# Grouping GpSimd's weight additions and tying each group to a point of VectorE's work

## The chip, the cores and the metric

The kernel runs on one core of a Trainium2 chip. The metric is the device time of one execution in microseconds (us); several executions of a kernel are timed and their median is taken. The engines of a core are TensorE (PE in the profile, with its weight loads as PEld), VectorE (DVE), ScalarE (ACT), GpSimd (POOL) and the DMA issuer SyncE (SP). They run side by side, each in the order of its own program, and wait for each other only where the data require it.

## What is computed

For x of shape 2 x 2048 x 512 in float32, two layers follow each other, cut here to what matters:

```python
def dense(x, wi, wo): return relu(x @ wi) @ wo          # 512 -> 2048 -> 512
s0, s1 = dense(x, swi[0], swo[0]), dense(x, swi[1], swo[1])
eo     = dense(x, wi[type_label], wo[type_label])       # weights picked per batch row
w      = softmax(relu(concat(eo[:,0], s0[:,0], s1[:,0]) @ g1) @ g2)
x      = x + eo*w[0] + s0*w[1] + s1*w[2]
out    = x + (x @ W[cat_ids] + b[cat_ids])
```

## The kernel before

**Units.** The tokens are cut into four blocks of 1024. A unit is one block with one pair of weights (one expert): four blocks with shared expert 0 (units 0 to 3), four with shared expert 1 (units 4 to 7), and four with the two experts that the labels pick (units 8 to 11; two blocks each). Each unit has an up part (x times wi, L755) and a down part (h times wo, L886).

**Seven products in place of eight.** Both parts are done as a two-level Strassen-Winograd scheme: seven outer products, and in each of them seven inner ones. This saves matmuls, and needs sums of quarters of the operands in exchange. An up product has 14 slots (`SEQ_UP`) of two matmuls, in the order i = 1, 6, 2, 5, 7, 4, 3; the down part has 49 slots (`SLOTS_DN`) of four matmuls, in the order i = 1, 2, 3, 7, 6, 5, 4. A slot's name such as "x6" or "y5" gives the accumulation bank (x, y or z) and the inner product that is added to it.

**Who makes the sums.** VectorE adds the results of the banks together, since the scheme's outputs are sums of partial results (L772, L778, L783, L796, L802 in the up part; L900, L908, L910, L917, L919 in the down part). These read one operand from the accumulation banks and one from SBUF. It also makes the sums of the hidden values: `wide` (L733) and `make_tops` (L690 to L697) in the up part, `outer_sum` (L857), `make_tops` and `y_sums` (L863) in the down part; these read both operands from SBUF. GpSimd makes the sums of x for the next products (`x_sums`, L356 and L370, in the up parts of units 0 to 4 and the ends of the down parts before them), and the sums of the weights of the next experts.

**The weight additions.** Class `Prep` makes the weight sums of one expert and one kind (up or down weights). There are six such objects (experts 1 to 3, two kinds), and each works in four groups of twelve additions (`line`, issued at L141): four of 128x384 elements for tile `po`, four of 128x512 for `ps`, four of 128x512 for `pt`. So there are 288 additions. A group's raw weights are loaded into one buffer by eight DMAs on SP's queue (L179); each finished tile is stored to DRAM by SP three slots later (`flush`, L228), and fetched as weight tiles by later units through a ring of twelve buffers (`fetch_w`, `wp`).

**The pacing.** The program is written out slot by slot. At the end of each slot, `prep_paced` (L637) advances a clock and adds a rate to a balance, and for each whole unit of the balance it issues one weight addition into GpSimd's program:

```python
        pace[0] = min(pace[0] + rate, 4.0) if prep_bg else 0.0
        while prep_bg and pace[0] >= 1 and prep_step():
            pace[0] -= 1
    ...
    RATE_UP = [0.36, 0.34, 0.34, 0.34, 0.18, 0.18, 0.34]
    RATE_DN = {1: 0.0, 2: 0.0, 3: 0.1, 7: 0.4, 6: 0.0, 5: 0.25, 4: 0.45}
```

This sets the order within GpSimd's program and the place of the raw loads and stores in SP's program. It does not bind the additions to VectorE or TensorE in time: an addition starts as soon as GpSimd reaches it and its operands are there. Other work that is issued at each slot's end stands beside it: `advance(xg, 1)` (x sums, before the pacing in the same slot), `next(tg, None)` and `next(job, None)` (VectorE's sums).

Of the kernel before, what the change touches and what calls it, by code (L numbers as in the profile page):

```python
# [8 lines left out]
F32 = mybir.dt.float32  # L9
# [10 lines left out]
ADD, SUB = ALU.add, ALU.subtract  # L20
# [16 lines left out]
def cond_resid_kernel(  # L37
# [22 lines left out]
    nc = tc.nc  # L60
# [10 lines left out]
    const = ctx.enter_context(tc.tile_pool(name="const", bufs=1))  # L71
# [72 lines left out]
    class Prep:  # L144
# [89 lines left out]
        def step(self):  # L234

            self.flush(clock[0])
            done = bool(self.p) and (len(self.p) != 12 or clock[0] >= self.since + 6)
            if done:
                self.p.pop(0)()
            self.more()  # L240
            return done

        def more(self):
            if self.reading == 0 and (not self.p or clock[0] >= self.free):
                self.begin()
# [86 lines left out]
    def fetch_parts(n, i):  # L332

        t = xp.tile([P, NP, TQ], F32, tag="xr", name=f"xs_{n}_{i}")
        nc.sync.dma_start(out=t, in_=xs[units[n][1]][:, i - 1])
        for k in PART_B:
            x_ops[n, i, k] = t[:, PART_B[k], :]
# [99 lines left out]
    clock = [0]  # L437
# [175 lines left out]
    def used_w():  # L613
        w_used[0] += 1
        fetch_w(w_used[0] + 12)
# [3 lines left out]
    prep_bg, other_bg = [], []  # L619
# [9 lines left out]
    def prep_step():  # L629
        done = prep_bg[0].step()  # L630
        if prep_bg[0].over():
            prep_bg.pop(0)
        return done

    pace = [0.0]

    def prep_paced(rate):  # L637
        clock[0] += 1
        if prep_bg:
            prep_bg[0].flush(clock[0])  # L640
        pace[0] = min(pace[0] + rate, 4.0) if prep_bg else 0.0
        while prep_bg and pace[0] >= 1 and prep_step():
            pace[0] -= 1

    def advance(gen, count=None):

        while count is None or count > 0:
            mark = next(gen, "next")
            if mark:
                return True  # L650
            if count is not None:
                count -= 1
        return False
# [6 lines left out]
    def blk_of(t, cc):  # L660

        r, q = INNER[cc]
        o = (r * 2 + q) * 1024
        return t[:, o : o + 1024].rearrange("p (g t) -> p g t", g=NG)
# [35 lines left out]
    def up(n, xg, tops, y):  # L700
# [12 lines left out]
        for j, i in enumerate(I_UP(n)):  # L713
# [11 lines left out]
            def relu(q, cc):  # L725
                v = blk_of(O[q], cc)
                nc.scalar.activation(v, v, AF.Relu)  # L727

            def wide(q, cc):


                o = blk_of(O[q], cc)
                nc.vector.tensor_tensor(o, blk_of(O[22], cc), blk_of(O[21], cc), ADD)  # L733
                if q == 22:
                    relu(22, cc)
# [6 lines left out]
            done = False  # L742
# [3 lines left out]
            for s, (bk, k, d) in enumerate(SEQ_UP):  # L746
                first = (bk, k) in (("x", 1), ("y", 5))
                if first:
                    bank[bk, d] = ps.tile(
                        [P, 2, TQ], F32, tag=bk, name=f"u{bk}_{n}_{i}_{d}"  # L750
                    )
                p = bank[bk, d]
                wt = w_tiles[n, 0, i, k]
                for g in range(2):
                    nc.tensor.matmul(  # L755
                        p[:, g, :],
                        lhsT=wt[:, 2 * d + g, :],
                        rhs=x_ops[n, i, k],
                        start=first and g == 0,
                        stop=True,  # L760
                        skip_group_check=True,
                    )
                if all(kk != k for _, kk, _ in SEQ_UP[s + 1 :]):
                    used_w()
                if k == 1:
                    z = bank["z", d] = ps.tile(
                        [P, 2, TQ], F32, tag="z", name=f"uz_{n}_{i}_{d}"
                    )
                    if store:
                        nc.scalar.activation(z, p, AF.Copy)  # L770
                    else:
                        nc.vector.tensor_tensor(z, p, half(src, 11, d), ADD)  # L772
                elif bk == "x" and k in SNAP:
                    t = snp.tile([P, 2, TQ], F32, tag="sn", name=f"us_{n}_{i}_{k}_{d}")
                    if store:
                        nc.scalar.activation(t, p, AF.Copy)  # L776
                    else:
                        nc.vector.tensor_tensor(  # L778
                            t, p, half(src, 12 if k == 6 else 22, d), ADD
                        )  # L780
                    sn[SNAP[k], d] = t
                    if k == 7:
                        nc.vector.tensor_tensor(  # L783
                            half(dst, 22, d), bank["y", d], t, ADD
                        )
                        if d == 1 and i in final:
                            relu(dst, 22)
                elif bk == "z":
                    nc.scalar.activation(  # L789
                        half(dst, 11, d), p, AF.Relu if i in final else AF.Copy  # L790
                    )
                elif k == 4:
                    if store:
                        nc.scalar.activation(half(dst, 21, d), p, AF.Copy)
                    else:
                        nc.vector.tensor_tensor(  # L796
                            half(dst, 21, d), p, half(src, 21, d), ADD
                        )
                    if d == 1 and i in final:
                        relu(dst, 21)  # L800
                elif k == 3:
                    nc.vector.tensor_tensor(half(dst, 12, d), p, sn["b", d], ADD)  # L802
                    if d == 1 and i in final:
                        relu(dst, 12)
                if s in wides:
                    wide(*wides[s])
                if n == 0 and i == 2:

                    for cc in {1: (11, 22), 2: (21,), 3: (12,)}.get(s, ()):
                        nc.scalar.activation(blk_of(O[21], cc), blk_of(O[11], cc), AF.Copy)  # L810
                if n == 0:
                    begin.outer({(1, 0): (5,), (1, 2): (6,), (2, 2): (7,), (6, 2): (3,)}.get((i, s), ()))
                    if (i, s) == (2, 2):
                        begin.second()
                    elif (i, s) == (7, 3):
                        begin.outer2(2)
                if xg and j < 6 and not done and (
                    s >= 7 if i in (7, 4) else s % 2 == 0 or j == 0
                ):
                    done = advance(xg, 1)  # L820
                if s in top_at:
                    next(tg, None)
                prep_paced(RATE_UP[j])
                step(other_bg)
                if s == 4 and n not in MAKES and j + 2 < NP:
                    fetch_parts(n, I_UP(n)[j + 2])
# [8 lines left out]
    def down(n, H, tops, y, prepare):  # L835
# [24 lines left out]
        def y_sums(m2, *pairs):  # L860
            for q, r in pairs:
                o = quad_of(y, q)[:, m2, :]
                nc.vector.tensor_tensor(o, o, quad_of(y, r)[:, m2, :], ADD)  # L863
# [96 lines left out]
        for s, (i, name) in enumerate(SLOTS_DN):  # L960
            if s in at:
                for _ in job:
                    pass
                job = jobs[at[s]]()
                y_sums(0, *sums.get(at[s], ()))
            elif s in second:
                y_sums(1, *sums.get(second[s], ()))
            slot(i, name)
            next(job, None)
            if name == "z2" and i != 1:  # L970
                next(job, None)
            prepare(s)
            prep_paced(RATE_DN[i])
            step(other_bg)
        for _ in job:
            pass
# [192 lines left out]

    RATE_UP = [0.36, 0.34, 0.34, 0.34, 0.18, 0.18, 0.34]
    RATE_DN = {1: 0.0, 2: 0.0, 3: 0.1, 7: 0.4, 6: 0.0, 5: 0.25, 4: 0.45}

    with tc.manual_schedule():

# [15 lines left out]
        for n, (e, blk) in enumerate(units):  # L1192
# [4 lines left out]
            if n:  # L1197
                y = yp.tile([P, DC, 4, TQ], F32, tag="y", name=f"y_{n}")
            H = up(n, xg, tops, y)
            coming = {}  # L1200

            def prepare(s, n=n, y=y):
# [30 lines left out]
                elif s in (30, 38):  # L1233
                    fetch_parts(m, I_UP(m)[(s - 30) // 8])

            down(n, H, tops, y, prepare)
            if n + 1 < len(units):
                xg = coming.get("s")
# [45 lines left out]
```

## Time and profile before

| | |
|---|---|
| median of three executions | 2267.57 us (2265.73 to 2278.35) |
| the profiled execution | 2271.67 us |
| its span in the profile | 2269.9 us |
| PE busy | 2200.9 us (97%) |
| DVE busy | 1662.7 us (73%) |
| POOL busy | 790.4 us (35%) |
| granted TensorE clock, mean | 0.994 |
| weight additions (L141) | 288, in units 0 (end) to 8 |

The profiled execution took 2271.67 us, 1.8 us more than its span and 4.1 us more than the median. A busy time is the sum of an engine's instructions; in a list of waits, the engine on the left stood still for what is on the right. In a list by form, "x16 | 19.2, 1217" means sixteen instructions, 19.2 us of busy time, 1217 ns for one on average. In a timeline, a line may merge several instructions; its two numbers are the start and the duration in us.

### The profile page before, as it was taken

How to read it: one execution, taken by the hardware profiler on the slowest of the kernel's cores; microseconds unless marked ns; L12 is line 12 of the kernel's file. 1: busy time of each engine (PE TensorE's matmuls, PEld its weight loads, DVE VectorE, ACT ScalarE, POOL GpSimd, SP SyncE). 2: the span in 40 equal slices, each digit the busy share in tenths (PEclk: the TensorE clock that was granted, in tenths of full speed). 3: DMA queues.
4: the chain of work that ended last, by engine and by line, in shares of the span. 5: the costliest groups of instructions: out<-in, count | busy, mean ns of one | idle time of the engine just before them, and what ended most of it. 6: DMA issues, size and time to landing. Idle time of an engine off the chain costs nothing.

```text
span 2269.9 us, 28541 instructions
## 1 busy us (share of the span) xinstructions
PE 2200.9 (97%) x9808; PEld 1852.3 (82%) x9808; DVE 1662.7 (73%) x2010; ACT 545.0 (24%) x937; POOL 790.4 (35%) x598
## 2 busy tenths in 40 slices
PE   7899999999999999899999999999999999999999
PEld 6787888888888888788888888888877877887676
DVE  7798687577598688588588588577676746857685
ACT  3221231331321231141131131131133133213310
POOL 5777642651751752333054134230032023002300
PEclk9999999999999999999999999999999999999999
DMA  9543997997996897796896896896896697579671
GB/s 320 213 148 110 334 337 219 327 310 231 329 329 207 285 330 213 255 323 200 284 327 178 280 327 207 280 327 174 283 312 187 185 301 244 153 242 326 208 273 56
DMA packets 479691, 577.22 MB, mean 254 GB/s; under 512 B 28216, under 2 KB 311864, under 8 KB 475580
## 3 DMA queue, kind: packets, MB, share of 16 engines
q1 hardware_dynamic: 475276, 567.53, 77.5%
q10 hardware_dynamic: 4272, 7.87, 1.0%
q8 instruction: 80, 1.31, 0.2%
q14 instruction: 63, 0.52, 0.1%
HBM read 417.47 MB, written 157.81 MB: 253 GB/s over the span
## 4 chain that ended last, share of the span: by engine, by line
PE 77%; DVE 14%; DMA 4%; issue 2%; POOL 2%; SPq 1%; ACT 0%; DVEq 0%; POOLq 0%; ACTq 0%
PE ux L755 21%; PE dx L886 20%; PE dy L886 10%; PE uy L755 10%; PE dz L886 5%; PE uz L755 5%; PE po L1066 5%; DVE h L857 2%; DVE h L733 2%; DVE y L863 1%; DVE t L690 1%; DVE t L695 1%; DVE t L693 1%; DMA g1raw<-in_L_cond_g_dram 1%; DMA y<-in_L_cond_swi_dram 1%
## 5 line engine op out<-in xcount | busy, mean ns | idle before, releaser
L886 PE MATMUL dx<-t,w 128*128 128x256 f32 x1680 | 399.0, 380 | 10.2 <-DVE ds L908 9.9
L755 PE MATMUL ux<-xs,w 128*128 128x256 f32 x1568 | 376.7, 381 | 11.4 <-DVE sm L1029 3.2
L886 PEld LDWEIGHTS dx<-t,w 128*128 128x128 f32 x1680 | 318.1, 190 | 58.6 <-DVE ds L908 12.3
L755 PEld LDWEIGHTS ux<-xs,w 128*128 128x128 f32 x1568 | 295.1, 190 | 67.8 <-DVE us L778 8.3
L1103 POOL TENSOR_TENSOR mix<-mix 128x512 f32<-128x512 f32 x72 | 101.9, 1416 | 532.9 <-DMA w<-ws_t 325.6
L141 POOL TENSOR_TENSOR po<-pr 128x384 f32<-128x384 f32 x48 | 58.9, 1241 | 601.4 <-DMA w<-ws_t 269.2
L778 DVE TENSOR_TENSOR us<-ux,h 128x512 f32<-128x512 f32 x240 | 162.5, 686 | 122.1 <-PE ux L755 121.8
L857 DVE TENSOR_TENSOR h<-h,h 128x1024 f32<-128x1024 f32 x192 | 251.2, 1323 | 0.0
L727 ACT ACTIVATE h<-h 128x1024 f32<-128x1024 f32 x156 | 164.5, 1056 | 245.1 <-DVE h L783 111.1
L783 DVE TENSOR_TENSOR h<-uy,us 128x512 f32<-128x512 f32 x168 | 116.0, 691 | 121.4 <-ACT us L776 117.0
L755 PE MATMUL ux<-xi,w 128*128 128x256 f32 x808 | 194.2, 384 | 9.6 <-issue 3.5
L789 ACT ACTIVATE h<-uz 128x512 f32<-128x512 f32 x168 | 99.6, 593 | 378.7 <-PE uz L755 354.5
L755 PE MATMUL uy<-xs,w 128*128 128x256 f32 x784 | 187.7, 380 | 2.7 <-DVE h L802 2.4
L755 PEld LDWEIGHTS ux<-xi,w 128*128 128x128 f32 x808 | 153.8, 192 | 36.5 <-issue 8.3
L886 PE MATMUL dy<-h,w 128*128 128x256 f32 x672 | 162.3, 385 | 12.1 <-DVE y L910 12.1
L755 PEld LDWEIGHTS uy<-xs,w 128*128 128x128 f32 x784 | 148.4, 190 | 29.1 <-DVE h L802 5.1
L886 PEld LDWEIGHTS dy<-h,w 128*128 128x128 f32 x672 | 128.2, 192 | 32.9 <-DVE y L910 10.4
L733 DVE TENSOR_TENSOR h<-h,h 128x1024 f32<-128x1024 f32 x96 | 148.3, 1545 | 6.7 <-ACT h L789 5.4
L802 DVE TENSOR_TENSOR h<-uy,us 128x512 f32<-128x512 f32 x168 | 113.0, 687 | 51.6 <-PE uy L755 49.4
L886 PE MATMUL dz<-h,w 128*128 128x256 f32 x616 | 145.6, 379 | 0.1
L886 PE MATMUL dx<-h,w 128*128 128x256 f32 x616 | 145.5, 379 | 0.0
L886 PE MATMUL dy<-t,w 128*128 128x256 f32 x576 | 136.1, 379 | 0.0
(153 smaller groups left out, 3359.1 us busy)
## 6 DMA issues: line engine op xcount, KB each, us to landing
w<-ws_t SPq DMA_DIRECT2D x352, 256.0 KB, 4.4
w<-ws_s SPq DMA_DIRECT2D x270, 256.0 KB, 4.2
w<-ws_o SPq DMA_DIRECT2D x264, 256.0 KB, 5.0
xs<-xs SPq DMA_DIRECT2D x49, 896.0 KB, 6.9
ws_s<-ps SPq DMA_DIRECT2D x24, 1024.0 KB, 9.9
ws_t<-pt SPq DMA_DIRECT2D x24, 1024.0 KB, 7.7
ys<-y SPq DMA_DIRECT2D x11, 2048.0 KB, 8.7
ws_o<-po SPq DMA_DIRECT2D x24, 768.0 KB, 7.5
```

The source lines that it names most:

```text
L141: eng.tensor_tensor(o, i0, i1, op)
L727: nc.scalar.activation(v, v, AF.Relu)
L733: nc.vector.tensor_tensor(o, blk_of(O[22], cc), blk_of(O[21], cc), ADD)
L755: nc.tensor.matmul(p[:, g, :], lhsT=wt[:, 2 * d + g, :], rhs=x_ops[n, i, k], start=first and g == 0, stop=True, skip_group_check=True,)
L778: nc.vector.tensor_tensor(t, p, half(src, 12 if k == 6 else 22, d), ADD)
L783: nc.vector.tensor_tensor(half(dst, 22, d), bank["y", d], t, ADD)
L789: nc.scalar.activation(half(dst, 11, d), p, AF.Relu if i in final else AF.Copy)
L802: nc.vector.tensor_tensor(half(dst, 12, d), p, sn["b", d], ADD)
L857: nc.vector.tensor_tensor(bl(o), bl(i0), bl(i1), SUB)
L886: nc.tensor.matmul(p, lhsT=wt[:, g, :], rhs=op[g], start=first and g == 0, stop=True, skip_group_check=True,)
L1066: nc.tensor.matmul(po[t], lhsT=mixed[c], rhs=l1[blk][0][:, c, :], start=(c == 0), stop=(c == DC - 1),)
L1103: nc.gpsimd.tensor_tensor(m[:, 3, :, :], m[:, 3, :, :], m[:, j, :, :], ADD)
```

## The change

The pacing is split in two. `prep_tick` runs at every slot and only advances the clock and stores what is due. `prep_run` issues a group of additions at the slots that two tables name, and, if an addition can be issued, puts a one-element memset into VectorE's program first and a one-element addition that reads it into GpSimd's program. GpSimd's program is in order, so everything behind that small addition waits until VectorE has come to the memset. The memsets take turns over 64 columns of a tile. A balance (`debt`, at most 4) carries what could not be issued; a group holds at most one addition more than its table says.

```diff
+        def can(self):
+            return bool(self.p) and (len(self.p) != 12 or clock[0] >= self.since + 6)
...
-    pace = [0.0]
-
-    def prep_paced(rate):
+    PULSES = 64
+    pulse = const.tile([1, PULSES], F32, name="pulse")
+    seen = const.tile([1, 1], F32, name="seen")
+    pulses, debt = [0], [0]
+
+    def prep_tick():
         clock[0] += 1
         if prep_bg:
             prep_bg[0].flush(clock[0])
-        pace[0] = min(pace[0] + rate, 4.0) if prep_bg else 0.0
-        while prep_bg and pace[0] >= 1 and prep_step():
-            pace[0] -= 1
+
+    def prep_run(count):
+
+        if not prep_bg:
+            return
+        debt[0] = min(debt[0] + count, 4)
+        most = count + 1
+        ready = False
+        while prep_bg and debt[0] and most:
+            if prep_bg[0].can() and not ready:
+                k = pulses[0] % PULSES
+                pulses[0] += 1
+                mark = pulse[:, k : k + 1]
+                nc.vector.memset(mark, 0.0)
+                nc.gpsimd.tensor_tensor(seen, mark, mark, ADD)
+                ready = True
+            if not prep_step():
+                break
+            debt[0] -= 1
+            most -= 1
...
-                prep_paced(RATE_UP[j])
+                prep_tick()
+                prep_run(RUN_UP[j].get(s, 0))
...
-            prep_paced(RATE_DN[i])
+            prep_tick()
+            prep_run(RUN_DN.get((i, name), 0))
...
-    RATE_UP = [0.36, 0.34, 0.34, 0.34, 0.18, 0.18, 0.34]
-    RATE_DN = {1: 0.0, 2: 0.0, 3: 0.1, 7: 0.4, 6: 0.0, 5: 0.25, 4: 0.45}
+    RUN_UP = [{4: 3, 8: 2}] * 3 + [{4: 2, 8: 2}] * 4
+    RUN_DN = {(7, "y5"): 2, (5, "x6"): 2, (4, "x6"): 2, (4, "z2"): 1}
```

More of the change, by code (lines that the diff above doesn't have):

```diff
@@ L236, in step @@
             self.flush(clock[0])
-            done = bool(self.p) and (len(self.p) != 12 or clock[0] >= self.since + 6)
+            done = self.can()
             if done:
```

## The prediction

> **What bounds the kernel now.** First the page: the span, the busy times, and how PE stands to the span.
>
> ```profile
> span 2269.9 us, 28541 instructions
> PE 2200.9 (97%) x9808; PEld 1852.3 (82%) x9808; DVE 1662.7 (73%) x2010; ACT 545.0 (24%) x937; POOL 790.4 (35%) x598
> ```
>
> PE is the bound: all but 69 us of the span. The change touches no matmul, so what can be won is PE's idle time where weight additions run. I cut the span into the up and down parts of units 1 to 8 (221.5 to 1620.6 us) and asked for the busy times of each. Two rows, unit 4's down part and unit 8's (after the duration: PE, PEld, DVE, ACT, POOL busy, granted clock, DMA share, GB/s):
>
> ```profile
> 836.60:930.80 94.20, 87.59 (x394) 76.06 (x393) 70.90 (x76) 9.88 (x25) 21.65 (x12) 0.96 0.68 208
> 1536.00:1620.60 84.60, 84.60 (x393) 74.47 (x393) 62.85 (x76) 10.06 (x25) 0.00 (x0) 1.00 0.60 180
> ```
>
> Unit 8's down has no GpSimd work and no PE idle time. Unit 4's has twelve weight additions and is 9.6 us longer: 6.6 us idle, and 3.0 us of longer PE time behind it at a granted clock of 0.96. Over the sixteen parts, span less PE busy is 1399.1 - 1373.5 = 25.6 us: the downs of units 1 to 7 have 1.2, 0.5, 1.1, 6.6, 1.2, 1.8 and 2.3 (14.6), the eight ups 11.0. PE's waits from 221.5 to 1536 us say for what:
>
> ```profile
> PE dy L886 <- DVE y L910: 7.1, 3, 6.3
> PE dx L886 <- DVE ds L908: 6.7, 7, 1.6
> PE ux L755 <- issue: 3.5, 5, 1.1
> PE ux L755 <- DVE uz L772: 2.3, 3, 1.5
> PE ux L755 <- DMA w<-in_L_cond_swi_dram: 2.1, 1, 2.1
> PE ux L755 <- POOL xi L370: 0.9, 2, 0.7
> ```
>
> Mostly for a late VectorE. (An "issue" wait of 1.1 us ends at 629.2 us, where VectorE's L772 ends at 629.1: that is VectorE too.) Why it is late stands in the timeline of unit 4's long wait:
>
> ```profile
> 905.82 2.17 DVE L693 TENSOR_TENSOR t<-h,t 128x1024 f32<-128x1024 f32 x1
> 906.87 2.25 POOL L141 TENSOR_TENSOR ps<-ps,pr 128x512 f32<-128x512 f32 x1
> 907.91 2.28 DVE L695 TENSOR_TENSOR t<-h 128x1024 f32<-128x1024 f32 x1
> 909.20 2.12 POOL L141 TENSOR_TENSOR ps<-pr,ps 128x512 f32<-128x512 f32 x1
> 916.13 1.65 PE L886 MATMUL dy<-h,w 128*128 128x256 f32 x3 [6.30 <-DVE y L910]
> ```
>
> GpSimd and VectorE alternate, each twice as long as alone: without GpSimd (unit 8's down) these VectorE forms take 1217 to 1223 ns, and a 128x512 addition alone takes 1.23 us from start to start. So an addition that meets a two-SBUF-operand VectorE sum costs VectorE 2.28 - 1.22 = 1.06 us. The additions come in bursts of about twelve, as soon as a raw load lands; this burst met nine VectorE sums in a row. The up part's plain sums (one operand from the banks) are not stretched: 687 ns on average everywhere.
>
> **The change, part by part.**
>
> *Count.* Following the old balance and the new tables slot by slot through the code, both issue 37 or 38 additions a unit and come to the 288th in unit 8's up part (old in its last product, new in its fifth), so none is left to be forced at the end. The new program has 143 groups, 18 to 20 in a full unit. A unit has 31 additions in its up part and 7 in its down part by the tables. In the trace the old program executes 29, 31, 29, 29, 24, 24, 25, 24 in the ups and 8, 6, 9, 12, 12, 12, 11 in the downs, since GpSimd runs out of step with the slots. Nothing is removed; additions move from downs to ups and into short groups.
>
> *Added on VectorE: 143 memsets.* No such memset is in the trace. Nearest rows: a 128x4 copy (L983) takes 158 ns; from below, 128x512 sums start every 0.60 us and 128x1024 ones every 1.13, so the part that does not grow is 2 x 0.60 - 1.13 = 0.07 us. The Trainium skill ("VectorE: DVE Perf Modes", the section on where the cycles go for N=2048) speaks against many small instructions: some 150 cycles of each are start-up, (1 + 150) / 0.96 GHz = 0.157 us. By the rule 143 cost 22.5 us of VectorE, by the start-to-start rows 10 us. I take the row, as the memsets follow other work without a wait. Most lie where VectorE waits for PE next (it idles 27% of the span) and cost nothing; about two a unit stand in a row of sums that PE may wait for: 16 x 0.16 = 2.5 us at most. A gain from the memset itself is excluded: it does no work that anything needs sooner.
>
> *Added on GpSimd: 143 one-element additions and waits.* 256 elements take 0.69 us from start to start, 512 take 1.23: fixed part 2 x 0.69 - 1.23 = 0.15 us, 21 us in all, on an engine that is 35% busy. The wait: a reader starts about 0.06 us after VectorE's writer ends (L910 ends 916.07, PE starts 916.13). Behind a waiting GpSimd stand its additions and, in units 1 to 4, the x sums that PE needs; see the second rival.
>
> *Moved: where the groups fall in the downs.* Unit 8's down shows VectorE's free places, since nothing disturbs it:
>
> ```profile
> 1578.09 1.22 DVE L695 TENSOR_TENSOR t<-h 128x1024 f32<-128x1024 f32 x1
> 1581.54 0.42 DVE L910 TENSOR_TENSOR y<-dy,ds 128x256 f32<-128x256 f32 x1 [2.23 <-ACT ds L906]
> ...
> 1604.72 1.41 DVE L863 TENSOR_TENSOR y<-y 128x512 f32<-128x512 f32 x2
> 1606.05 1.22 DVE L697 TENSOR_TENSOR t<-h,t 128x1024 f32<-128x1024 f32 x1
> ...
> 1607.52 0.42 DVE L900 TENSOR_TENSOR dz<-dx,y 128x256 f32<-128x256 f32 x1
> ```
>
> (7, "y5"): the memset follows L695 (ends 1579.3), then VectorE waits 2.2 us for PE. Two additions, 0.06 + 0.15 + 2 x 1.23 = 2.7 us, fit but for 0.2 us after L910's short sum. (5, "x6"): the memset stands before L863 at 1604.72, in the densest row of the part; two additions delay L900 by 2 x 1.06 + 0.16 + 0.15 = 2.4 us, from 1607.9 to 1610.3. PE's next "x6" on that bank is slot 43, at 1536.0 + 43 x 84.6/49 = 1610.2: a wait of 0 to 0.3 us. (4, "x6"): the two L863 behind it are delayed by the same 2.4, the next L908 has 1.65 us of idle time before it, so it is 0.8 us late, and PE comes back to its bank one slot (1.73 us) later. (4, "z2"): one addition before 2.57 us of idle time. So a down should lose 0.4 us: 7 x 0.4 = 3 us where now 14.6 - 0.4 (a DMA wait for x) + 3.0 (slow clock) = 17.2 are lost. Gain 14.
>
> *In the ups.* In the products i = 1, 6, 2 VectorE has no two-SBUF sums: fifteen of 31 additions are free. In i = 5, 7, 4, 3 the slot-4 pairs fall on one-operand sums, except i = 5's (one `make_tops` sum, with slack behind); the slot-8 pairs end 12 us into a 12.1 us product and meet the wide sums of slots 11 to 13. In i = 5 that pushes L772 of the next product by about 0.5 us beyond PE's need. Now the ups lose 11.0 - 2.1 (DMA) = 8.9 us; I put 0.8 a part for after, 6.4. Gain 2.5.
>
> *SP.* Stores and raw loads stay three slots behind or with the next group; a store that waits some 2 us for a gated group holds up weight fetches that run twelve tiles, 12 x 1.73 = 21 us, ahead, and land in 4.4 us. Cost nothing; without that lead it would be the 2 us each.
>
> *Sum.* -14 - 2.5 + 2.5 = -14 us against the profiled execution's own 2271.67, giving 2257.7; it stood 4.1 us above the median of the runs, to which the same -14 gives 2253.6. I predict 2254.
>
> **Rivals.**
>
> *The stalls only move.* For: the gate brings additions into a dense row in every down and up, where bursts hit only some (downs of units 2 and 3 lost 0.5 and 1.1 us). If (5, "x6") costs 1.5 us in seven downs and i = 5 and 7 cost 1.5 in eight ups, that is 22 us for today's 26, less with memsets: within 4 us, 2264 to 2270. Against: 1610.3 against 1610.2 leaves it near zero, and hardly a group is over three.
>
> *GpSimd comes late with x (slower).* In the ups of units 1 to 4 GpSimd has 26 x sums beside 31 additions and can no longer run ahead. Place: i = 7, where the sums for i = 4 are issued at slots 7 to 10 around the second pair. VectorE reaches the memset of slot 8 at about 9 x 0.864 + 2 x 0.6 = 9.0 us, the pair ends at 11.7, the sum for k = 7 at 12.4; PE needs it at slot 7 of the next product, 12.1 + 6.0 = 18.1. Slack 5.7 us. It decides if additions stretch to 2.25 us (2 us lost a pair) and two more pairs pile up. Then three products in each of four units lose some 2.5 us: +30, with the gain 2267.6 - 14 + 30 = 2284. For: PE waits 1.3 us for POOL already (0.9 and another 0.4). Against: the slack.
>
> *The gate does nothing*: if GpSimd always comes to the mark later than VectorE, bursts remain; 2266 to 2270. Against: it idles 65% of the span, and in the downs it is free.
>
> **How the numbers follow.** A difference under 0.5% (11.3 us) can't be told from no change here. Forecast (2254; 2243 to 2262, from losing almost nothing to half of the stalls staying): 0.60. Stalls move: 0.22. Gate does nothing: 0.05. GpSimd late, or the memsets all on the path (+22.5): 0.13. Of the forecast's own range, about 0.52 lies below 2256.2; the rest, with the first and third cases, makes 0.35 within 0.5%; 0.13 slower. The range is 2242 (17.2 + 8.9 us won, nothing paid) to 2270.
>
> **What would show it.** Right: unit 4's down at 85 us; L857, L690 to L697 near 1.22 us but for L697 and L863 behind "x6" of i = 5; the downs' idle time at about 3 us in sum; memsets of 0.07 to 0.16 us. Wrong: PE waits for POOL xi over 5 us, L910 or L908 waits in every down near slot 43, or L141 groups longer than four.

## The result, and the profile after

The changed kernel takes 2276.35 us (median of 22 executions, 2269.99 to 2280.73), the kernel before 2269.93 us (22 executions, 2265.59 to 2278.35). The ratio is 1.0025, 95% interval 1.0017 to 1.0034: slower by a quarter of a per cent, which is less than the 0.5% that I had called measurable (with 22 executions the interval still leaves out 1), outside of my range, and not the gain that I forecast.

The profiled execution took 2271.38 us, 5.0 us less than the median. Its page looks like that of before:

```profile
span 2269.6 us, 28874 instructions
PE 2200.5 (97%) x9808; PEld 1854.9 (82%) x9808; DVE 1647.7 (73%) x2153; ACT 544.8 (24%) x937; POOL 772.5 (34%) x741
```

Equal spans hide two large differences. Cut by parts, in us, each from where TensorE's first matmul of the part starts to where the next part's does:

| part | before | after | difference |
|---|---|---|---|
| unit 0 (unchanged up to its last slot) | 211.3 | 206.2 | -5.1 |
| ups of units 1 to 3 | 261.9 | 280.9 | +19.0 |
| ups of units 4 to 8 | 432.1 | 430.5 | -1.6 |
| downs of units 1 to 7 | 620.5 | 608.6 | -11.9 |

Unit 0 took between 206 and 211 us in all profiles of this study, with the same work, so its 5.1 us are an accident of two executions: in it the granted clock was 0.50 for 20.4 us before and for 13.6 us after, which makes about 3.4 of them. The other three lines make +5.5 us, in accord with the medians (+6.4).

So the down parts lost less, as was forecast. The ups of units 1 to 3 lost more than they won. The busy times of these three ups before (columns as in the prediction):

```profile
221.50:308.00 86.50, 85.59 (x393) 74.07 (x392) 60.43 (x80) 29.40 (x42) 61.83 (x54) 1.00 0.97 321
397.90:486.30 88.40, 85.51 (x393) 74.03 (x392) 60.25 (x79) 29.43 (x42) 65.48 (x58) 1.00 0.95 309
576.00:662.90 86.90, 85.17 (x394) 74.15 (x393) 61.83 (x80) 29.43 (x42) 61.30 (x56) 1.00 1.01 331
```

After, with unit 4's down as the last row:

```profile
216.50:310.40 93.90, 87.80 (x393) 75.08 (x392) 65.49 (x94) 29.28 (x42) 64.41 (x72) 0.98 0.95 316
400.20:495.20 95.00, 89.39 (x393) 76.50 (x392) 66.64 (x95) 29.35 (x42) 66.50 (x78) 0.95 0.96 312
584.70:676.70 92.00, 87.75 (x394) 75.95 (x394) 66.13 (x96) 29.41 (x42) 72.64 (x79) 0.96 0.96 317
848.90:934.30 85.40, 84.82 (x393) 74.37 (x392) 66.98 (x81) 9.96 (x25) 11.87 (x13) 1.00 0.74 228
```

Unit 4's down fell from 94.2 to 85.4 us: the long wait and the low clock behind it are gone. In the three ups TensorE idles 4 to 6 us each, and its time grows by 2 to 4 us more at a granted clock of 0.95 to 0.98, as it did behind unit 4's wait before. Its waits from 216.5 to 1536.5 us:

```profile
PE dy L910 <- DVE y L934: 7.4, 7, 1.3
PE uy L778 <- issue: 6.1, 2, 5.0
PE uy L778 <- POOL xi L373: 4.1, 1, 4.1
```

The waits for a late L908 (now L932) are gone. Each down now has one short wait for L934 (the old L910). New are one of 5.0 us (unit 2's up) and one of 4.1 us (unit 3's up). Unit 1's up, which grew most (7.4 us), has no long wait but five of 2.1 us and less, 6.1 us in sum; the longest ends behind a VectorE sum of 3.82 us. Unit 3's wait shows itself plainly. SP's own row of that up part first, then the timeline:

```profile
644.89 0.53 SPq L228 DMA_DIRECT2D ws_t<-pt  x1
645.85 3.03 SPq L472 DMA_DIRECT2D w<-ws_t  x2
649.10 4.50 SPq L179 DMA_DIRECT2D pr<-in_L_cond_wi_dram  x8
```

```profile
657.43 1.57 POOL L141 TENSOR_TENSOR po<-pr 128x384 f32<-128x384 f32 x1 [6.36 <-DMA w<-ws_s]
...
661.28 1.86 POOL L141 TENSOR_TENSOR po<-pr,po 128x384 f32<-128x384 f32 x1
663.10 0.72 POOL L373 TENSOR_TENSOR xi<-x 128x256 f32<-128x256 f32 x1
...
663.87 3.78 PE L778 MATMUL uy<-xi,w 128*128 128x256 f32 x8 [4.14 <-POOL xi L373]
```

The raw load (L179) stands in the program at slot 9 of i = 7, where TensorE is at 641.2 us. Ahead of it on SP's queue stands the store L228, which waits for a gated addition until 644.9, and the load starts at 649.1, 7.9 us late. The wait of the store is 2.7 us of this, the two weight fetches behind it 3.0 us; why these take so long, the trace doesn't show. The seventh of the load's eight DMAs lands at 656.7. The first addition of these data is due six slots behind the load, and GpSimd stands still for 6.36 us at it, with an x sum behind it; then four additions pass (that one and three more), and the x sum that TensorE needs comes at 663.1. (The profile names another DMA as the releaser, `ws_s`; the raw load fits: its eighth DMA was issued 0.6 us behind the seventh, and by the same time to landing it would land at about 657.3, an estimate.)

The 5.0 us in unit 2's up begin with the same wait (5.5 us for a raw load, until 441.4 us), but end in another way:

```profile
445.93 8.71 DVE L756 TENSOR_TENSOR h<-h,h 128x1024 f32<-128x1024 f32 x1 [0.23 <-ACT h L812]
...
446.31 0.71 POOL L373 TENSOR_TENSOR xi<-x,xi 128x256 f32<-128x256 f32 x1
...
452.31 1.25 POOL L141 TENSOR_TENSOR ps<-ps,pr 128x512 f32<-128x512 f32 x1
453.64 2.13 POOL L141 TENSOR_TENSOR ps<-pr,ps 128x512 f32<-128x512 f32 x1
```

One wide sum of VectorE takes 8.71 us. Nine GpSimd operations, each at its undisturbed length, pass it in a row from 446.31 to 453.56 us, three additions, four sums of inner and outer x parts and two readers of marks among them. At 453.64 a GpSimd operation that reads the result of the one before it comes, with a pause of 78 ns ahead, and VectorE gets in: it is done at 454.6, L825 behind it at 455.25, and TensorE starts at 455.35, after what the profile calls "issue". In the burst of before that the prediction shows, the engines alternated. Elsewhere, in unit 4's up, the trace of before had a passed sum too, with five GpSimd operations in a row:

```profile
787.59 6.11 DVE L690 TENSOR_TENSOR y<-h 128x1024 f32<-128x1024 f32 x1 [1.12 <-DMA w<-ws_s]
```

### The profile page after: what moved, and what is told of

It is laid out like the page before. It is cut to its first block, busy times and chain, and to the rows that moved or that the text cites. A ratio compares the mean times of both kernels' runs of the same rounds, so it can differ in the third digit from the quotient of the medians.

```text
span 2269.6 us, 28874 instructions
## 1 busy us (share of the span) xinstructions
PE 2200.5 (97%) x9808; PEld 1854.9 (82%) x9808; DVE 1647.7 (73%) x2153; ACT 544.8 (24%) x937; POOL 772.5 (34%) x741
## 4 chain that ended last, share of the span: by engine, by line
PE 77%; DVE 12%; DMA 2%; issue 2%; POOL 1%; ACT 0%; SPq 0%; DVEq 0%; ACTq 0%
PE dx L910 20%; PE ux L778 20%; PE dy L910 11%; PE uy L778 10%; PE dz L910 5%; PE uz L778 5%; PE po L1091 5%; DVE h L756 2%; DVE y L887 1%; DVE h L881 1%; DVE t L718 1%; DVE t L713 1%; DVE t L716 1%; DMA g1raw<-in_L_cond_g_dram 1%; DVE hid L1031 1%
## 5 line engine op out<-in xcount | busy, mean ns | idle before, releaser
L910 PE MATMUL dx<-t,w 128*128 128x256 f32 x1680 | 397.3, 379 | 1.6 <-DVE ds L932 1.6
L910 PEld LDWEIGHTS dx<-t,w 128*128 128x128 f32 x1680 | 318.2, 190 | 46.4 <-DVE ds L932 2.6
L661 POOL TENSOR_TENSOR seen<-pulse 1x1 f32<-1x1 f32 x143 | 41.9, 293 | 703.7 <-DVE pulse L660 697.0
L778 PE MATMUL ux<-xi,w 128*128 128x256 f32 x808 | 195.7, 386 | 11.8 <-DVE us L801 4.2
L910 PE MATMUL dy<-h,w 128*128 128x256 f32 x672 | 161.3, 383 | 13.4 <-DVE y L934 13.4
L910 PEld LDWEIGHTS dy<-h,w 128*128 128x128 f32 x672 | 127.4, 191 | 34.7 <-DVE y L934 10.8
L825 DVE TENSOR_TENSOR h<-uy,us 128x512 f32<-128x512 f32 x168 | 112.9, 686 | 50.8 <-PE uy L778 48.6
L910 PE MATMUL dz<-h,w 128*128 128x256 f32 x616 | 145.6, 379 | 0.1
L910 PE MATMUL dx<-h,w 128*128 128x256 f32 x616 | 145.5, 379 | 0.0
L910 PE MATMUL dy<-t,w 128*128 128x256 f32 x576 | 136.1, 379 | 0.0
```

What stands on the lines that cost most here:

```text
L661: nc.gpsimd.tensor_tensor(seen, mark, mark, ADD)
L778: nc.tensor.matmul(p[:, g, :], lhsT=wt[:, 2 * d + g, :], rhs=x_ops[n, i, k], start=first and g == 0, stop=True, skip_group_check=True,)
L910: nc.tensor.matmul(p, lhsT=wt[:, g, :], rhs=op[g], start=first and g == 0, stop=True, skip_group_check=True,)
```

## The experiments

Theory A: the gate wins in the down parts, and loses in the ups of units 1 to 3, where x sums stand behind gated additions. Rivals: B, each memset and reader costs a little wherever it stands; C, the tables and not the gate put additions, loads and stores at bad places. Small ratios with their intervals are against the kernel before on the same chip. Sums of parts are taken from each run's profile, as in the table above.

**Half of it: units 4 to 8 only.**

```diff
-                prep_tick()
-                prep_run(RUN_UP[j].get(s, 0))
+                if n >= 4:
+                    prep_tick()
+                    prep_run(RUN_UP[j].get(s, 0))
+                else:
+                    prep_paced(RATE_UP[j])
```

(The same in the down part; `prep_paced` and the old rates come back.)

> Groups tied to VectorE in units 4 to 8 only, the old rates in units 1 to 3. Theory A (the gate wins in the down parts, and loses in the up parts of units 1 to 3, where the x sums stand behind it in GpSimd's queue): the down parts of units 4 to 7 win 10.8 us and the up parts of units 4 to 8 win 1.7, as in the profile after, so about 2270 - 12 = 2258 us, ratio 0.9945. Theory B (each memset and its reader costs a little wherever it stands): 85 of 143 pulses remain, so slower than before by over half of the change's 6 us, about 2273 us.

2256.26 us, 0.9951 (0.9937 to 0.9965). The three up parts take 262.1 us, as before, and the downs 608.9. A holds, B does not.

**The other half: units 1 to 3 only** (`n < 4`).

> The other half: groups tied to VectorE in units 1 to 3 only. Theory A: the up parts of units 1 to 3 lose 19 us and their down parts win 1, so about 2288 us, ratio 1.008; with the other half's kernel the two differences add up to the change's own 6 us. Theory B: 58 of 143 pulses, about 2272 us.

2284.53 us, 1.0080 (1.0063 to 1.0096). The two halves, -0.49% and +0.80%, add up to +0.31% against the change's +0.25%. This run also tells how far a single profile can be trusted: the same three ups, gated in the same way, took 275.1 us in its profiled execution (2278.41 us, the fastest of six) and 280.9 in the change's. Without the gate (before, the first half, and three of the kernels below) they took 261.3 to 262.7 us.

**The tables without the gate.**

```diff
-                mark = pulse[:, k : k + 1]
-                nc.vector.memset(mark, 0.0)
-                nc.gpsimd.tensor_tensor(seen, mark, mark, ADD)
```

> The new tables and balance, without the memset and without its reader, so nothing ties the groups to VectorE. Theory A: GpSimd runs ahead again; the stalls of the down parts come back (some 12 us against the change) and the loss in the up parts of units 1 to 3 goes (19 us), so within 5 us of before, 2266 to 2275 us. Theory C (the loss comes from where the tables put the additions, raw loads and stores in the queues, not from the gate): the up parts of units 1 to 3 still lose over 10 us, 2280 us or more.

2265.79 us, 0.9988 (0.9978 to 0.9998). The ups of units 1 to 3 are back at 262.7 us, and unit 4's and unit 5's downs have long waits again (4.7 and 2.7 us idle). So C falls for the loss: it is the gate that loses. For the gain it holds in part. The downs of units 1 to 7 take 615.2 us here, some 5 us less than before, so by these profiles nearly half of the change's 11.9 us came with the tables and the rest with the gate.

**More memsets.** To the first half's kernel, two more memsets ahead of each group.

```diff
-                nc.vector.memset(mark, 0.0)
+                for _ in range(3):
+                    nc.vector.memset(mark, 0.0)
```

> The tied groups in units 4 to 8 only, with three memsets in place of one ahead of each group, so 170 more memsets on VectorE. If a memset costs VectorE 0.07 us and lies beside VectorE's waits for PE nearly everywhere, at most 2 us more than the 2256 us of the kernel with one, so 2256 to 2258. If each costs PE 0.16 us [...], 170 x 0.16 = 27 us more: 2283.

2257.54 us, 0.9949 (0.9936 to 0.9963), where the kernel with one memset had 0.9951. 170 more memsets cost nothing that can be seen. In the trace a memset takes 59 ns.

**The place in the down part.** To the first half's kernel:

```diff
-    RUN_DN = {(7, "y5"): 2, (5, "x6"): 2, (4, "x6"): 2, (4, "z2"): 1}
+    RUN_DN = {(7, "y5"): 2, (4, "x1"): 2, (4, "x7"): 3}
```

> The tied groups in units 4 to 8 only, and in the down part at other places: two additions behind slot (4, x1) and three behind (4, x7), where VectorE next waits for PE, in place of the pairs behind (5, x6) and (4, x6). In the kernel without this move each down part of units 4 to 7 still loses 0.6 to 1.3 us to a late L934 behind the (5, x6) pair, 4.2 us in sum. If that pair is the cause, these waits go: about 2252 us, ratio 0.993. If they are no matter of place (any two additions hold VectorE up somewhere), it stays at 2256 us, 0.995.

2255.09 us, 0.9934 (0.9921 to 0.9948). The downs of units 4 to 7 take 338.4 us for 344.0, with no idle time of TensorE at all; the interval still meets that of the kernel without the move, and the ups of units 4 to 8 took 434.7 us for 430.3 in the two profiles (one waits 2.0 us for a weight tile). Whether that is chance or a cost of the move, this run doesn't tell; in the last kernel below, which has the same places, they took 431.3.

**The first addition later.** The change, with

```diff
-            return bool(self.p) and (len(self.p) != 12 or clock[0] >= self.since + 6)
+            return bool(self.p) and (len(self.p) != 12 or clock[0] >= self.since + 14)
```

> The change, with the first addition of each group of twelve held back for 14 slots behind the issue of its raw load, not 6. Theory A1 (in the up parts of units 1 to 3 GpSimd stands at additions whose raw weights have not landed, and x sums queue up behind them): GpSimd's waits for the loads go, and the 19 us lost in these up parts fall to under 8: 2259 to 2266 us. Theory A2 (the gate and the x sums alone fill GpSimd there, loads or not): at most 4 us better than the change, 2272 us or more.

2270.12 us, 1.0005 (0.9994 to 1.0016), between the times of the two theories. GpSimd's waits for raw loads in the ups of units 1 to 3 fall from 25.7 us to 4.9, and these ups from 280.9 to 270.8 us. So by these two profiles 10.1 of the 19.0 us were the late loads: about half, and less than I expected. The later additions also cost something further on: unit 8's down takes 86.1 us for 84.6 and unit 9's up 121.3 for 118.6, where TensorE waits 3.4 us for VectorE's L825. VectorE sums of 3.7 and 5.2 us remain in units 1 and 2.

**Who passes whom.** Three small kernels for the lock between the two engines, my word for whatever makes a GpSimd addition and a two-SBUF-operand VectorE sum wait for each other. The first has 2, 4 or 8 additions on GpSimd behind a memset, and six two-SBUF-operand sums on VectorE:

> A small kernel that copies x to the output and leaves all of the computation out; it measures who waits for whom when GpSimd's additions (128x512) and VectorE's two-SBUF-operand sums (128x1024, 1.22 us alone) meet. Behind one memset stand 2, 4 or 8 additions on GpSimd; on VectorE 0, 1 or 3 one-operand sums (0.6 us each) and then six two-operand ones. If the engines alternate (as in the burst of unit 4's down part before), the first two-operand sum takes at most 2.5 us in every case, and with eight additions all six take about 2.3. If a sum that comes while GpSimd runs is locked out until GpSimd's run ends, the first sum takes about 1.2 + what is left of the run: 3 us with two additions and one sum ahead, 5.5 us with four, 10 us with eight, 8.5 us with eight and three ahead, and the other five take 1.22.

The engines alternated in all cases: sums of 1.2 to 2.3 us, whether they came before GpSimd's run or into it. In the second kernel the sums have to wait for something first:

> A small kernel that copies x to the output and leaves all of the computation out. In the first one the engines always alternated, while in the whole kernel some VectorE sums were passed by 2 to 10 GpSimd operations. Here eight additions stand behind each memset, and VectorE's two-SBUF-operand sums wait for something first: for the sum before (a chain in place), for a sum of another tile (a pair), for a one-operand sum, or for ScalarE. If a sum that has had to wait comes to the lock only when GpSimd's run holds it, it is passed by several additions (4 us and more for one sum); if waiting makes no difference, every sum takes at most 2.4 us.

The same: no sum over 2.4 us. In both kernels each addition wrote the same place as the one before it. In the third they write eight places:

```diff
-                for _ in range(8):
-                    nc.gpsimd.tensor_tensor(g, ga, gb, ADD)
+                for q in range(8):
+                    nc.gpsimd.tensor_tensor(g[:, q, :], ga, gb, ADD)
```

> A small kernel that copies x to the output and leaves all of the computation out. In the first two small kernels each addition of GpSimd wrote over the one before it, and the engines always alternated. In the whole kernel the passing ended where a GpSimd operation reads or follows the one just before it (a pause of 78 ns), or where GpSimd had to wait. Here the eight additions write eight different places, so that no pause stands between them. If the pause is what lets VectorE in, a two-SBUF sum that comes into the run is passed by all that is left of it: 9 to 10 us for the first sum, and 1.22 us (0.69 for 512 elements) for the others. If not, the engines alternate as before, at most 2.4 us a sum.

One round of its first case, in its timeline:

```profile
26.10 17.14 DVE L54 TENSOR_TENSOR vra<-srca,srcb 128x1024 f32<-128x1024 f32 x6
...
27.33 9.78 POOL L51 TENSOR_TENSOR gra<-gina,ginb 128x512 f32<-128x512 f32 x8
```

Eight additions run through in 9.78 us. Of the six sums the first takes 1.22 us, the second 10.84 us, the others 1.22 again. Additions to one place, in the first kernel, stand 78 ns apart, also where no sum is waiting; additions to eight places start 1.22 us apart, 0.03 us before the one ahead has ended. So a run without pauses can keep VectorE out to its end, and a run with pauses let it in at each. But not always: where the first two-SBUF sum came into the middle of the run, behind one-operand sums, the engines alternated here too (1.9 to 2.2 us a sum), and where it waited for ScalarE both happened. What decides between the two, beyond the order in which they meet, stays open.

**A pause behind each addition.** The change, with

```diff
             eng.tensor_tensor(o, i0, i1, op)
+            one = o[0:1, 0, 0:1] if len(o.shape) == 3 else o[0:1, 0, 0, 0:1]
+            eng.tensor_tensor(rest, one, one, ADD)
```

> The change, with a one-element addition behind each of GpSimd's weight additions that reads what the addition wrote, so that GpSimd pauses there and VectorE can take the lock. Theory L (in the up parts of units 1 and 2 VectorE's sums are passed by 3 to 10 GpSimd operations in a row, and that is the part of the loss that a later first addition did not take away): no VectorE sum over 2.6 us there, and 4 to 8 us faster than the change: 2267 to 2271 us. Theory M (GpSimd is simply short of time there): the 288 pauses of some 0.25 us add 8 us of GpSimd work to each of these up parts, and it gets worse, 2280 us or more.

2278.10 us, 1.0044 (1.0030 to 1.0058), for the change's 1.0025 (1.0017 to 1.0034). Only one VectorE operation over 2.6 us is left between 205 and 1600 us, where the change had twelve. Yet the ups of units 1 to 3 take 280.9 us, as in the change's profile. TensorE's waits:

```profile
PE uy L782 <- POOL xi L377: 14.9, 4, 5.7
```

What it had waited for a locked-out VectorE it now waits for late x sums. Theory L's 2267 to 2271 us were missed, and M's 2280 us all but reached. The pauses take GpSimd's time as well (each 0.15 us from start to start behind a pause of 0.08 us, some 30 in an up), so this run alone doesn't tell whether the lock-out cost nothing of its own or whether its gain went into the pauses.

**The pause and the later first addition.**

> The same pause, and the first addition of a group of twelve held back for 14 slots behind its raw load. Under theory L with theory A1 (late raw loads) the two causes are apart and their gains add: the up parts of units 1 to 3 come within 4 us in sum of before, so 2259 to 2265 us. Under theory M: no better than the later first addition alone, 2270 us or more.

2264.33 us, 0.9974 (0.9966 to 0.9983). The ups of units 1 to 3 take 266.5 us, 4.3 less than with the later first addition alone. Here the pause pays: with the first additions later, ending the lock-out won more than the pauses cost (in the ratios 0.31%, some 7 us). So M falls. Up by up, unit 3's came back with the later addition alone (91.9 us in the change, then 87.4; before 86.9), unit 2's only with the pause (95.1, then 92.4, then 87.4; before 88.5), and unit 1's with neither (93.9, 91.1, 92.1; before 86.5). 4.6 us against before are left, in unit 1's up, where TensorE still waits 3.9 us for x sums.

**All three together.**

> The same, with the down part's groups at the free places: two behind (4, x1) and three behind (4, x7). The down parts of units 1 to 8 lose some 1.2 us each to the pair behind (5, x6) in the kernel with the later first addition; these 9 us go: 2250 to 2257 us under theory L, 2262 or more under theory M.

2250.51 us, 0.9921 (0.9907 to 0.9934): the fastest of the study, ahead of both kernels. Its ups of units 1 to 3 take 263.4 us. In its downs of units 1 to 8 TensorE is never idle: 88.1 us in units 1 and 2, which have some 32 more matmuls, and 84.6 us in the others. Unit 4's:

```profile
829.40:914.00 84.60, 84.60 (x394) 74.57 (x393) 63.19 (x79) 9.97 (x25) 12.95 (x18) 1.00 0.72 224
```

VectorE's time is nearly that of a down without any additions (62.85 in the prediction's row of unit 8). The downs of units 1 to 8 take 683.8 us, 12.6 less than without the move (9 expected).

## Why the prediction was wrong

*The downs* were right in direction and nearly in size: -14 forecast, -11.9 measured. In part this was luck: nearly half of it came with the tables alone, and the forecast had put all of it to the gate. My 0.4 us a down for what remains was mis-sized; the wait for L934 is 7.4 / 7 = 1.05 us. The delay was right (2.4 forecast), the consumer was wrong. I looked for TensorE's next need of the x bank, in slot 43, but the next need is slot 42, "y3" of i = 5 on the y bank, whose last reader is that L934:

```profile
1089.17 2.48 POOL L141 TENSOR_TENSOR ps<-pr 128x512 f32<-128x512 f32 x2
1089.20 3.01 DVE L887 TENSOR_TENSOR y<-y 128x512 f32<-128x512 f32 x1
...
1093.27 0.41 DVE L934 TENSOR_TENSOR y<-dy,ds 128x256 f32<-128x256 f32 x1
...
1093.74 1.13 PE L910 MATMUL dy<-h,w 128*128 128x256 f32 x4 [1.27 <-DVE y L934]
```

In unit 5's down, L887 waits for both additions in a row (3.01 us for 0.69), L934 comes 2.3 us later than in an undisturbed down, and 1.27 us of that reach TensorE. The moved groups confirm it: with them the wait is gone.

*The memsets* were over-priced: 59 ns in the trace, where the rule that I cited makes 157, and tripling them cost nothing visible. I wrote that I take the row of 0.07 us and yet reckoned the 2.5 us with 0.16. "2.5 us at most" should have been near 0. The reader on GpSimd takes 183 ns undisturbed, and what follows starts 0.15 us after it does, as I took it.

*The ups of units 4 to 8* were right (-1.6; the 2.5 us were for all eight).

*The step that failed is the slack of 5.7 us in the rival that GpSimd comes late with x, and with it "SP ... cost nothing".* The sum behind that slack lets GpSimd start at i = 7 on time and has no term for the raw load. Under *SP* I asked only what a store that waits for a gated group holds up, and named the weight fetches, which have 21 us of lead. The raw load stands in the same queue, and its first addition is due as little as six slots, 5.2 us, behind it, where the load alone takes 6 to 8 us from issue to landing and starts 2.9 to 12.5 us after TensorE has come to its slot. So in the ups of units 1 to 3 GpSimd started on five of six such groups 7.6 to 11.8 us behind TensorE, and the slack was gone.

The stores that I had asked about are the smaller part of this: they waited 2.1 and 2.7 us ahead of unit 3's two loads, and at most 0.6 us ahead of the late loads of units 1 and 2. The loads of before started as late (2.6 to 12.5 us after TensorE's slot), and GpSimd came to their first additions up to 9.3 us behind TensorE. But then it went through what stood behind them at its own speed. The gate makes it stand at marks, time that it then lacks; in unit 1's up 23.9 us (the row), in unit 2's 22.1, in unit 3's only 6.6, where the loads took 11.6:

```profile
POOL seen L661 <- DVE pulse L660: 23.9, 7, 5.7
```

I had given the case of a late GpSimd 0.13, together with the memsets, and put 30 us to it, from stretched additions; it came, with 19.0 us, and took back more than the downs and the other ups won. Of these, by single profiles, 10.1 us are the loads (shown by holding the first addition back), 4.3 the lock-out (shown by the pause on top of that), and 4.6 remain. The sizes are rough, as the 275.1 us of the half change show; the ratios, each against before, go the same way (1.0025, 1.0005, 0.9974). That the 4.6 us are GpSimd's lack of time in unit 1 is read from one profile and was not tried by itself.

*Not foreseen:* that additions can pass a waiting VectorE sum one after another. I had priced each meeting at 1.06 us from a burst in which the engines alternated; the sum of 6.11 us, in the same trace, would have shown the other case.

## What to carry to other kernels

When an engine is gated to another's progress, go through all that stands behind the gate, in its own queue (here the x sums) and in each queue that waits for it (here a store on SP, and the load behind that store), and compare each one's lead with the whole delay: a gate takes away the running ahead that had hidden a load's latency. Place groups where the other engine next waits, not where it is busy, and find the consumer by the very next use of each bank. When spans agree, cut them by stage before believing in no effect: here +19.0 and -13.5 us cancelled to a quarter of a per cent.

## What the runs showed of the hardware

A run of GpSimd additions (128x512, 1.22 us from start to start) that write different places kept a two-SBUF-operand VectorE sum waiting for all eight of them (10.84 us for a sum of 1.22 us), a wait that no data required; eight that write the same place, 78 ns apart, let one sum in after each (2.2 us a sum). The Trainium skill ("SBUF — State Buffer", the section on who interferes with whom) calls the ports that these two engines share an exclusive lock, for which a VectorE instruction with two SBUF inputs contends with a GpSimd instruction that reads SBUF. If the engines took turns at it, a sum would wait for one addition of 1.25 us and take about 2.5 us at most, an estimate from the rows here. The alternating cases agree with that, the 10.84 us do not: the wait can be a whole run. In the whole kernel, the run of nine operations ended at a pause of 78 ns, ahead of an operation that reads the result of the one before it.

In the parts with TensorE's long waits its own time grew by 2 to 4 us on top of the wait. The granted clock was 0.50 for 6.8 us from 914.4 us on (unit 4's down before), and for 3.4 us from 289.7, 10.2 us from 453.6 and 6.8 us from 661.8 (the ups of units 1 to 3 after), and 1.00 in the rest of these parts.
